# Two-layer graph network: fixed slots for the layer-1 weights, every other part with its groups in reverse, and other prefetch distances

## Chip, cores and metric

The kernel runs on 1 core of one Trainium2 chip. The metric is the device time of one execution in microseconds, given as the median of several runs. The traces come from the hardware profiler, from one execution each; "span" is the time from the first to the last instruction of that execution.

## The reference, cut

Everything is float32. `x` is (128, 128, 256): 128 batches, 128 nodes, 256 features. `adj` is (128, 128, 128).

```python
# layer 0
h = max(layernorm(x), 0)                       # over the 256 features
conv = bn(conv1d_k1(h)); conv = relu(conv); conv = bn(conv1d_k17(conv))   # along the nodes
x_conv = relu(conv + h)
s = h @ w_se.T + b_se                          # 3 values a node
A = exp(-|s_n - s_m|^2) * adj
x_nmp = A @ relu(h @ w_msg.T + b_msg)
gi = concat(x_conv, x_nmp) @ w_ih.T + b_ih;  gh = h @ w_hh.T + b_hh       # a GRU cell
x = x + (1 - z) * tanh(gi_n + r * gh_n) + z * h        # r, z = sigmoid(...)

# layer 1: only nodes 0..24 of each batch change, in five overlapping groups
GROUPS = [25 nodes], [9 nodes], [7 nodes], [6 nodes], [6 nodes]
h = max(layernorm(x), 0)
for g in range(5):
    N_g = D^-1/2 (adj_g + I) D^-1/2            # D: row sums of adj_g + I
    y = relu(N_g @ (h_g @ W1[g]) + b1[g])      # 256 -> 512
    y = relu(N_g @ (y @ W2[g]) + b2[g])        # 512 -> 256
    fused[group g] += softmax(fusion_w)[g] * y
x = x + fused
```

## The kernel before

**Layer 0.** A front part computes the convolution (up to about 640 us). Then 32 blocks of four batches follow. The function `gates(i)` computes the GRU of block i, with TensorE matmuls written out in a fixed order (L505, L541); after each it calls `between()`, which takes one step of other work: in turn a step of `beside_gates(i + 1)` (messages L411, edges L431 to L447, the inverse of the convolution L394/L396, and `back(i - 1)`) and a step of the first unfinished layer-1 generator. `back` transposes the block's result (L572), adds the residual, and stores it with one queue, SyncE's: eight small stores of the rows that layer 1 needs into scratch `xg` (L579), and then one store of the other 103 rows of each of four batches to the output (L581). The `xt` tile is loaded at L811 and has two buffers.

**Layer 1.** The 128 batches are cut into parts of 32, 32, 32, 16, 8 and 8. When a part's blocks have gone through the gates, its generator `layer1(k)` is appended; every yield of it is one step. The last parts run after the last block has been stored. Each group's rows are cut into *packs* of at most 128 rows (several batches of s rows each), and packs are put together into *chunks* of at most 512 rows. A chunk goes through these stages:

- for each pack, `prepare(j)` and then the product of the normalized rows with the adjacency (L711), copied into `ax` (L712)
- for each group segment of the chunk, the product with `w1` (L728), with bias and Relu into `hh` (L733 on VectorE, L735 on ScalarE)
- for each pack, the product with `w2` (L745), copied to `s2` (L747); `last`, one pack later, multiplies by the adjacency again (L674) and applies bias, scale and Relu (L678). Group 0 writes the sum `f`, and the other groups write `og`, which VectorE adds to `f` (L685)

After its chunks a part loads the old rows (`x1`, L761), transposes `f` (L764), adds it (L765) and stores the output (L767).

`prepare(j)` runs ahead of its pack in three distances. Loads (adjacency rows `adj`, L595, and features `hg`, L597) are five packs ahead, `pack_rows` three, `pack_adj` one:

```python
            if 0 <= j + 5 < len(packs):
                loads[j + 5] = pack_load(k, *packs[j + 5])
            if 0 <= j + 3 < len(packs):
                g, _, nb = packs[j + 3]
                rows[j + 3] = pack_rows(g, nb, *loads.pop(j + 3))
            if 0 <= j + 1 < len(packs):
                g, _, nb = packs[j + 1]
                ready[j + 1] = pack_adj(nb * GROUPS[g][0], *rows.pop(j + 1))
```

`pack_rows` computes degrees (L608 to L611), the statistics of the layernorm (L612 `st`, L613), a power on GpSimd (L615 `pw`), the normalized rows (L618, L619) and the scaled block-diagonal adjacency `bd` (L621, L624). `pack_adj` transposes it (L630) and scales it into `nt` (L632).

The weights of a group, `w1` and `w2` of 512 KB each, are loaded by SyncE (L649) in each part anew: `w1` has two buffers and `w2` three, and the next load is issued when a group has been used for the last time. With five groups and six parts that is 60 loads.

The order of the work on each engine is the program's order. Tiles wait for buffers by semaphores. All loads and stores named here go through SyncE's queue, in program order; an instruction there that waits for a buffer holds what is behind it.

Of the kernel before, what the change touches and what calls it, by code (L numbers as in the profile page):

```python
# [8 lines left out]
F32 = mybir.dt.float32  # L9
# [4 lines left out]
P = 128  # L14
# [11 lines left out]
NN = 25  # L26
HID = 512
# [15 lines left out]
    return [(b[j], b[j + 1] - b[j]) for j in range(k)]  # L43


def _chunks(size):

    out, n = [], 513
    for g, (s, _) in enumerate(GROUPS):
        for b0, nb in _packs(size, s):  # L50
            if n + nb * s > 512:
                out.append([])
                n = 0
            out[-1].append((g, b0, nb))
            n += nb * s
    return out
# [10 lines left out]
def gnn_kernel(ctx: ExitStack, tc: tile.TileContext, io, out: bass.AP):  # L67
# [359 lines left out]
    def edge_terms(i):  # L427

        ps = bank()
        for k in range(2):  # L430
            nc.tensor.transpose(ps[:, k * P:(k + 1) * P], lr[:, k].rearrange("p b r -> p (b r)"), ident)  # L431
        lt = wk.tile([P, P], F32, tag="lt", name="lt", bufs=2)
        nc.scalar.copy(lt, ps[:, :P])
        rt = wk.tile([P, BB, N], F32, tag="rt", name="rt", bufs=1)
        nc.vector.tensor_tensor(rt, ps[:, None, P:2 * P].to_broadcast([P, BB, N]),
                                bmask[32][:, :, None].to_broadcast([P, BB, N]), op=ALU.mult)
        lrs[i] = lt, rt
# [152 lines left out]
    def pack_load(k, g, b0, nb):  # L590
        s = GROUPS[g][0]
        n = nb * s
        adj = l1.tile([P, NN], F32, tag="adj", name="adj", bufs=6)
        r0 = (first_of[k] + b0) * s
        nc.sync.dma_start(adj[:n, :s], io[f"adj{g}"][r0:r0 + n, :])  # L595
        hg = l1.tile([P, D], F32, tag="hg", name="hg", bufs=6)
        nc.sync.dma_start(hg[:n], xg[k][g][b0 * s:b0 * s + n, :])  # L597
        return adj, hg

    def pack_rows(g, nb, adj, hg):  # L600

        s = GROUPS[g][0]
        n = nb * s

        deg = l1.tile([P, 5], F32, tag="deg", name="deg", bufs=4)
        st = l1.tile([P, 6], F32, tag="st", name="st", bufs=4)
        pw = l1.tile([P, 4], F32, tag="pw", name="pw", bufs=4)
        nc.vector.reduce_sum(deg[:n, 0:1], adj[:n, :s], axis=AX.X)  # L608
        nc.vector.tensor_scalar(deg[:n, 0:1], deg[:n, 0:1], 1.0, None, op0=ALU.add)
        nc.vector.tensor_scalar(deg[:n, 1:2], deg[:n, 0:1], 0.0, None, op0=ALU.is_equal)  # L610
        nc.vector.tensor_add(pw[:n, 0:1], deg[:n, 0:1], deg[:n, 1:2])  # L611
        nc.vector.bn_stats(st[:n], hg[:n])  # L612
        nc.vector.bn_aggr(deg[:n, 2:4], st[:n])  # L613
        nc.vector.tensor_scalar(pw[:n, 1:2], deg[:n, 3:4], EPS, None, op0=ALU.add)  # L614
        nc.gpsimd.tensor_tensor(pw[:n, 2:4], pw[:n, 0:2], mhalf[:n, 0:2], op=ALU.pow)  # L615
        dinv = deg[:n, 4:5]
        nc.vector.tensor_sub(dinv, pw[:n, 2:3], deg[:n, 1:2])
        nc.vector.tensor_scalar(hg[:n], hg[:n], deg[:n, 2:3], pw[:n, 3:4], op0=ALU.subtract, op1=ALU.mult)  # L618
        nc.scalar.activation(hg[:n], hg[:n], AF.Relu)  # L619
        bd = l1.tile([P, P], F32, tag="bd", name="bd", bufs=3)  # L620
        nc.vector.scalar_tensor_tensor(  # L621
            bd[:n, :n].rearrange("p (b m) -> p b m", b=nb), adj[:n, None, :s].to_broadcast([n, nb, s]), dinv,
            bmask[s][:n, :nb, None].to_broadcast([n, nb, s]), op0=ALU.mult, op1=ALU.mult)
        nc.vector.scalar_tensor_tensor(bd[:n, :n], ident[:n, :n], dinv, bd[:n, :n], op0=ALU.mult, op1=ALU.add)  # L624
        return hg, bd, dinv

    def pack_adj(n, hg, bd, dinv):
# [4 lines left out]
        nc.vector.tensor_scalar(nt[:n, :n], pt[:n, :n], dinv, None, op0=ALU.mult)  # L632
        return hg, nt

    def layer1(k):
        size = PARTS[k]
        tag = "f" if size > 8 else f"f{size}"
        f = l1.tile([P, C, size if size <= 8 else max(PARTS), NN], F32, tag=tag, name=tag, bufs=1 if size > 8 else 2)
        chunks = _chunks(size)
        packs = [p for c in chunks for p in c]  # L640
        loads, rows, ready, late = {}, {}, {}, []
        w1s, w2s = {}, {}

        def weights(ws, name, key, bufs, shape, ahead):

            while len(ws) < min(len(GROUPS), ahead):
                g = len(ws)
                ws[g] = l1.tile(shape, F32, tag=name, name=name, bufs=bufs)
                nc.sync.dma_start(ws[g], io[key][g].rearrange("(c p) o -> p c o", p=P))  # L649

        def weights1(ahead):
            weights(w1s, "w1", "w1", 2, [P, C, HID], ahead)

        def weights2(ahead):
            weights(w2s, "w2", "w2", 3, [P, HID // P, D], ahead)

        def prepare(j):

            if 0 <= j + 5 < len(packs):
                loads[j + 5] = pack_load(k, *packs[j + 5])  # L660
            if 0 <= j + 3 < len(packs):
                g, _, nb = packs[j + 3]
                rows[j + 3] = pack_rows(g, nb, *loads.pop(j + 3))
            if 0 <= j + 1 < len(packs):
                g, _, nb = packs[j + 1]
                ready[j + 1] = pack_adj(nb * GROUPS[g][0], *rows.pop(j + 1))

        def last(g, b0, nb, s2, nt):

            s, runs = GROUPS[g]  # L670
            n = nb * s
            po = bank()
            for c in range(C):
                nc.tensor.matmul(po[:, c * P:c * P + n], s2[:n, c * P:(c + 1) * P], nt[:n, :n], start=True, stop=True)  # L674
            og = None if g == 0 else l1.tile([P, C, P], F32, tag="og", name="og", bufs=2)
            for c in range(C):
                dst = og[:, c, :n] if g else f[:, c, b0:b0 + nb, :].rearrange("p b m -> p (b m)")
                nc.scalar.activation(dst, po[:, c * P:c * P + n], AF.Relu, bias=nb2[:, g, c:c + 1], scale=nw[:, g:g + 1])  # L678
            if g:
                at = 0  # L680
                ov = og[:, :, :n].rearrange("p c (b m) -> p c b m", b=nb)
                for r0, rn in runs:
                    for c in range(C):
                        fv = f[:, c, b0:b0 + nb, r0:r0 + rn]
                        nc.vector.tensor_add(fv, fv, ov[:, c, :, at:at + rn])  # L685
                    at += rn

        for j in (-5, -4):
            prepare(j)
        yield  # L690
        weights1(2)
        weights2(3)
        for _ in range(8):
            yield
        for j in (-3, -2, -1):
            prepare(j)
            yield
        ends = {g: n + 1 for n, (g, _, _) in enumerate(packs)}
        j = 0
        for chunk in chunks:  # L700
# [3 lines left out]
            for g, b0, nb in chunk:  # L704
                n = nb * GROUPS[g][0]
                prepare(j)
                hg, nt = ready.pop(j)
                j += 1
                ps = bank()
                for c in range(C):  # L710
                    nc.tensor.matmul(ps[:, c * P:c * P + n], hg[:n, c * P:(c + 1) * P], nt[:n, :n], start=True, stop=True)  # L711
                nc.vector.tensor_copy(ax[:, :, at:at + n], ps[:, :C * P].rearrange("p (c m) -> p c m", c=C)[:, :, :n])  # L712
                work.append((g, b0, nb, nt, at))
                segs[g] = (segs[g][0] if g in segs else at, at + n)
                at += n
                if late:
                    last(*late.pop(0))
                yield j + 5 >= len(packs)
            hh = l1.tile([P, HID // P, 512], F32, tag="hh", name="hh", bufs=1)
            for g, (m0, m1) in segs.items():  # L720
                m = m1 - m0
                per = 2 if m <= 256 else 1
                for q0 in range(0, HID // P, per):
# [12 lines left out]
                    if late:  # L736
                        last(*late.pop(0))
                    if q0 + per == HID // P and j >= ends[g]:
                        weights1(g + 3)
                    yield  # L740
            for m, (g, b0, nb, nt, at) in enumerate(work):
                n = nb * GROUPS[g][0]
                ps = bank()
                for q in range(HID // P):
                    nc.tensor.matmul(ps[:n, :D], hh[:, q, at:at + n], w2s[g][:, q, :], start=q == 0, stop=q == HID // P - 1)  # L745
                s2 = l1.tile([P, D], F32, tag="s2", name="s2", bufs=3)
                nc.scalar.copy(s2[:n, :], ps[:n, :D])  # L747
                if late:
                    last(*late.pop(0))
                late.append((g, b0, nb, s2, nt))  # L750
                if j0 + m + 1 == ends[g]:
                    weights2(g + 4)
                yield
        while late:
            last(*late.pop(0))
# [1 line left out]

        n = BB * NN
        for b0 in range(0, size, BB):
            x1 = l1.tile([P, D], F32, tag="x1", name="x1", bufs=3)  # L760
            nc.sync.dma_start(x1[:n], xg[k][0][b0 * NN:b0 * NN + n, :])  # L761
            ps = bank()
            for c in range(C):
# [161 lines left out]
```

## Time and profile before

| what | value |
|---|---|
| median of three runs | 2194.7 us (2188.79, 2194.7, 2196.48) |
| the profiled run | 2192.57 us, span 2190.8 us, mean TensorE clock granted 0.965 |
| TensorE matmuls, busy | 2062.6 us, 94% of the span |
| VectorE, ScalarE, GpSimd, busy | 58%, 32%, 26% |
| DMA | 260.11 MB, of which 60 weight loads of 512 KB |
| chain that ended last | TensorE 73%, DMA 12%, VectorE 8%, GpSimd 3% |

A group's row gives line, engine, operation, shapes and count, then its busy time and the mean of one instruction, and then the idle time of the engine before it with what ended it. A row of waits gives the total, how often, and the longest. A float32 matmul runs as two passes, and the trace counts passes. A busy share of the whole says little about one stretch: the stretch up to 640 us (front part), the blocks, and the time after the last block have different limits.

### The profile page before, as it was taken

The page shows a single profiled execution, that of the slowest core. Times are in us where ns is not written, and L with a number is a line of the kernel's source. Part 1 is how long each engine was busy: PE and PEld are TensorE (multiplying, and loading weights), DVE is VectorE, ACT ScalarE, POOL GpSimd, SP SyncE. Part 2 cuts the span into 40 slices and gives each one's busy share as a digit, 9 for nine tenths or more (in the row PEclk, how much of TensorE's full clock was granted, in tenths as well). Part 3 has the DMA queues.
Part 4 walks back from the last instruction along what each step waited for, and adds up shares of the span by engine and source line. Part 5 has one row for each costly group of instructions (what it writes and reads, how often), then busy time and mean ns, then how long its engine had stood idle before and what let it go on. Part 6 is the DMA issues. An engine that isn't in the chain of part 4 may idle for free.

```text
span 2190.8 us, 31132 instructions
## 1 busy us (share of the span) xinstructions
PE 2062.6 (94%) x10981; PEld 1721.8 (79%) x10981; DVE 1274.0 (58%) x3518; ACT 697.7 (32%) x1424; POOL 580.0 (26%) x666
## 2 busy tenths in 40 slices
PE   7989979998999999999999999999999999998687
PEld 6878868887778778778888877888887788886576
DVE  6666447553556556576666657656665666655332
ACT  3433114311333233333333333333333333332222
POOL 3012521143323324232222422222242222222100
PEclk8889989999999999999999999999999999999786
DMA  8974964298322222221223222122322212221252
GB/s 318 337 261 162 305 225 153 106 297 263 118 65 63 77 67 60 72 75 57 82 86 103 71 72 75 57 81 87 102 71 73 74 55 82 81 77 48 64 158 68
DMA packets 200909, 260.11 MB, mean 119 GB/s; under 512 B 19378, under 2 KB 179378, under 8 KB 196146
## 3 DMA queue, kind: packets, MB, share of 16 engines
q1 hardware_dynamic: 192946, 220.37, 31.8%
q10 hardware_dynamic: 7808, 37.75, 4.5%
q8 instruction: 88, 1.44, 0.3%
q14 instruction: 67, 0.55, 0.1%
HBM read 175.63 MB, written 82.44 MB: 118 GB/s over the span
## 4 chain that ended last, share of the span: by engine, by line
PE 73%; DMA 12%; DVE 8%; POOL 3%; SPq 1%; issue 1%; ACT 1%; POOLq 0%; DVEq 0%; ACTq 0%
PE bank L505 27%; PE bank L269 6%; PE bank L541 5%; PE bank L728 5%; DMA hg<-xg 5%; PE bank L745 4%; DMA ln<-in_x_dram 4%; PE bank L202 3%; PE bank L264 3%; PE bank L411 3%; DMA out_dram<-xt 3%; PE bank L214 3%; PE bank L457 2%; PE bank L396 2%; PE bank L394 2%; PE bank L572 1%
## 5 line engine op out<-in xcount | busy, mean ns | idle before, releaser
L505 PE MATMUL bank<-t,sw 128*128 128x256 f32 x1024 | 253.9, 381 | 1.1 <-DVE nn L520 1.1
L518 POOL TENSOR_TENSOR u<-u,m 128x256 f32<-128x256 f32 x96 | 73.1, 762 | 635.2 <-ACT m L516 611.3
L505 PEld LDWEIGHTS bank<-t,sw 128*128 128x128 f32 x1024 | 187.5, 191 | 24.6 <-DVE nn L520 1.3
L505 PE MATMUL bank<-t,wih 128*128 128x256 f32 x768 | 197.8, 380 | 0.0
L505 PEld LDWEIGHTS bank<-t,wih 128*128 128x128 f32 x768 | 145.8, 190 | 34.1 <-issue 10.7
L728 PE MATMUL bank<-ax,w 128*128 128x192 f32 (+12 forms) x592 | 131.0, 374 | 25.7 <-DMA w<-in_w_dram 22.5
L728 PEld LDWEIGHTS bank<-ax,w 128*128 128x128 f32 x592 | 105.9, 223 | 43.4 <-issue 29.4
L202 PE MATMUL bank<-wc,ht 128*128 128x256 f32 x512 | 123.9, 397 | 17.0 <-ACT ht L193 13.1
L745 PE MATMUL bank<-w,hh 128*100 128x256 f32 (+8 forms) x552 | 136.8, 394 | 0.0
L261 POOL TENSOR_TENSOR vs<-v 128x512 f32<-128x512 f32 x78 | 101.6, 1322 | 128.7 <-DMA v<-vd 78.0
L615 POOL TENSOR_TENSOR pw<-pw,mhalf 100x2 f32<-100x2 f32 (+7 forms) x69 | 50.3, 729 | 301.1 <-DVE pw L614 153.2
L411 PE MATMUL bank<-wms,ht 128*128 128x259 f32 x512 | 124.8, 387 | 4.6 <-DMA ht<-htd 4.6
L202 PEld LDWEIGHTS bank<-wc,ht 128*128 128x128 f32 x512 | 98.3, 197 | 37.4 <-ACT ht L193 22.3
L541 PE MATMUL bank<-ht,whh 128*128 128x512 f32 x256 | 116.9, 600 | 0.0
L745 PEld LDWEIGHTS bank<-w,hh 128*100 128x100 f32 (+8 forms) x552 | 94.3, 173 | 28.3
L505 PE MATMUL bank<-xc,wih 128*128 128x256 f32 x384 | 114.8, 381 | 0.0
L505 PE MATMUL bank<-xn,wih 128*128 128x256 f32 x384 | 114.7, 380 | 0.0
L411 PEld LDWEIGHTS bank<-wms,ht 128*128 128x128 f32 x512 | 98.8, 193 | 20.2 <-issue 5.0
L259 DVE SCALAR_TENSOR_TENSOR s<-X 128x256 f32<-128x256 f32 x78 | 50.8, 653 | 90.6 <-PE bank L269 90.4
L415 ACT ACTIVATE msg<-msg 128x512 f32<-128x512 f32 x64 | 40.3, 630 | 197.1 <-DVE msg L412 185.0
L214 PE MATMUL bank<-fd,h 128*128 128x160 f32 x512 | 87.8, 332 | 15.0 <-ACT h L206 12.7
L214 PEld LDWEIGHTS bank<-fd,h 128*128 128x128 f32 x512 | 83.4, 215 | 17.8 <-ACT h L206 13.1
(175 smaller groups left out, 4391.0 us busy)
## 6 DMA issues: line engine op xcount, KB each, us to landing
v<-vd SPq DMA_DIRECT2D x80, 512.0 KB
w<-in_w_dram SPq DMA_DIRECT2D x60, 512.0 KB
vd<-sp SPq DMA_DIRECT2D x8, 2560.0 KB
yd<-ys ACTq DMA_DIRECT2D x40, 512.0 KB
ln<-in_x_dram SPq DMA_DIRECT2D x32, 512.0 KB
htd<-ht ACTq DMA_DIRECT2D x32, 512.0 KB
ht<-htd SPq DMA_DIRECT2D x32, 512.0 KB
ym<-yd SPq DMA_DIRECT2D x32, 512.0 KB
```

The costliest lines, as they stand in the source:

```text
L202: nc.tensor.matmul(pv[:, bb, :], ht[:, c, b * N:(b + 1) * N], wc1[:, c, :], start=c == 0, stop=c == C - 1)
L214: nc.tensor.matmul(ps[:, bb * 2 * LW:(bb + 1) * 2 * LW], h1[:, 2 * h + bb, c * P:(c + 1) * P], fd, start=True, stop=True)
L259: nc.vector.scalar_tensor_tensor(s, a, -2.0, d, op0=ALU.mult, op1=ALU.subtract)
L261: nc.gpsimd.tensor_tensor(vs, vr, vi, op=ALU.add)
L264: nc.tensor.matmul(p1[:, :D], a[:, c], vs[:, c], start=c == 0, stop=c == C - 1)
L269: nc.tensor.matmul(ps[:, k * D:(k + 1) * D], u[:, c], w[:, c], start=c == 0, stop=c == C - 1)
L411: nc.tensor.matmul(ps[:, :D + 3], ht[:, c, b * N:(b + 1) * N], wms[:, c, :], start=c == 0, stop=c == C - 1)
L505: nc.tensor.matmul(ps, w, d, start=n == 0, stop=n == len(pairs) - 1)
L518: nc.gpsimd.tensor_tensor(got["u4"], got["u2"], got["m5"], op=ALU.add)
L541: nc.tensor.matmul(ps, whh[:, c, col:col + P], ht[:, c, :], start=c == 0, stop=c == C - 1)
L728: nc.tensor.matmul(pv[:, q - q0, :], w1s[g][:, c, q * P:(q + 1) * P], ax[:, c, m0:m1], start=c == 0, stop=c == C - 1)
L745: nc.tensor.matmul(ps[:n, :D], hh[:, q, at:at + n], w2s[g][:, q, :], start=q == 0, stop=q == HID // P - 1)
```

## The change

- The weights get three fixed slots each for `w1` and `w2`: group g lies in slot g % 3. The first part loads groups 0, 1 and 2. When a group ends, the group three further on in the present direction is loaded into its slot.
- Odd parts run through the groups from 4 down to 0, so that three groups of each kind stay in place from one part to the next. There are 30 loads instead of 60. In odd parts `f` is first set to zero by GpSimd, and group 0 is added through `og` like the others.
- `prepare` runs six packs ahead for loads, four for `pack_rows` and two for `pack_adj`. The prologue of a part has one step more.
- Buffers: `hg` 6 to 7, `adj` 6 to 4, `bd` 3 to 2, `s2` 3 to 2, `x1` 3 to 2, `lt` 2 to 1. The slots take 24 KB a partition instead of 20.

```diff
-        lt = wk.tile([P, P], F32, tag="lt", name="lt", bufs=2)
+        lt = wk.tile([P, P], F32, tag="lt", name="lt", bufs=1)
...
-        adj = l1.tile([P, NN], F32, tag="adj", name="adj", bufs=6)
+        adj = l1.tile([P, NN], F32, tag="adj", name="adj", bufs=4)
...
-        hg = l1.tile([P, D], F32, tag="hg", name="hg", bufs=6)
+        hg = l1.tile([P, D], F32, tag="hg", name="hg", bufs=7)
...
-        bd = l1.tile([P, P], F32, tag="bd", name="bd", bufs=3)
+        bd = l1.tile([P, P], F32, tag="bd", name="bd", bufs=2)
...
+    w1s, w2s = {}, {}
+
+    def weights(ws, g):
+
+        if 0 <= g < len(GROUPS):
+            name, shape = ("w1", (D, HID)) if ws is w1s else ("w2", (HID, D))
+            ws[g] = l1.tile([P, shape[0] // P, shape[1]], F32, tag=f"{name}_{g % 3}", name=name, bufs=1)
+            nc.sync.dma_start(ws[g], io[name][g].rearrange("(c p) o -> p c o", p=P))
...
-        chunks = _chunks(size)
+
+        d = -1 if k % 2 else 1
+        chunks = _chunks(size, range(len(GROUPS))[::d])
...
-            if 0 <= j + 5 < len(packs):
-                loads[j + 5] = pack_load(k, *packs[j + 5])
-            if 0 <= j + 3 < len(packs):
-                g, _, nb = packs[j + 3]
-                rows[j + 3] = pack_rows(g, nb, *loads.pop(j + 3))
-            if 0 <= j + 1 < len(packs):
-                g, _, nb = packs[j + 1]
-                ready[j + 1] = pack_adj(nb * GROUPS[g][0], *rows.pop(j + 1))
+            if 0 <= j + 6 < len(packs):
+                loads[j + 6] = pack_load(k, *packs[j + 6])
+            if 0 <= j + 4 < len(packs):
+                g, _, nb = packs[j + 4]
+                rows[j + 4] = pack_rows(g, nb, *loads.pop(j + 4))
+            if 0 <= j + 2 < len(packs):
+                g, _, nb = packs[j + 2]
+                ready[j + 2] = pack_adj(nb * GROUPS[g][0], *rows.pop(j + 2))
...
-            og = None if g == 0 else l1.tile([P, C, P], F32, tag="og", name="og", bufs=2)
+            add = g or d < 0
+            og = l1.tile([P, C, P], F32, tag="og", name="og", bufs=2) if add else None
...
-        for j in (-5, -4):
+        for j in (-6, -5):
             prepare(j)
         yield
-        weights1(2)
-        weights2(3)
+        if k == 0:
+            for g in range(3):
+                weights(w1s, g)
+                weights(w2s, g)
+        if d < 0:
+            nc.gpsimd.memset(f, 0.0)
         for _ in range(8):
             yield
-        for j in (-3, -2, -1):
+        for j in (-4, -3, -2, -1):
             prepare(j)
             yield
...
-                yield j + 5 >= len(packs)
+                yield j + 6 > len(packs)
...
-                        weights1(g + 3)
+                        weights(w1s, g + 3 * d)
...
-                s2 = l1.tile([P, D], F32, tag="s2", name="s2", bufs=3)
+                s2 = l1.tile([P, D], F32, tag="s2", name="s2", bufs=2)
...
-                    weights2(g + 4)
+                    weights(w2s, g + 3 * d)
...
-            x1 = l1.tile([P, D], F32, tag="x1", name="x1", bufs=3)
+            x1 = l1.tile([P, D], F32, tag="x1", name="x1", bufs=2)
```

## The prediction

> **What bounds the kernel now.** I read the page first, then the windows by stage, the waits (TensorE's, the whole list, SyncE's queue), the chain in order of time, and last the timeline of the ends.
>
> ```profile
> PE 2062.6 (94%) x10981; PEld 1721.8 (79%) x10981; DVE 1274.0 (58%) x3518; ACT 697.7 (32%) x1424; POOL 580.0 (26%) x666
> ```
> ```profile
> 1755.00:1974.00 219.00, 214.84 (x1101) 178.25 (x1100) 133.02 (x386) 77.90 (x155) 54.05 (x67) 1.00 0.24 74
> 1974.00:2191.00 217.00, 168.54 (x815) 138.19 (x813) 85.99 (x360) 51.43 (x132) 26.52 (x34) 0.80 0.28 84
> 2050.00:2075.00 25.00, 6.23 (x50) 5.77 (x48) 7.23 (x40) 2.88 (x8) 1.40 (x2) 0.70 0.25 77
> ```
> The columns after the stretch are its length and the busy time of PE, PEld, DVE, ACT and POOL, then the granted clock, DMA share and GB/s. TensorE sets the time: from 640 to 1974 us, where blocks of layer 0 run with layer 1 between them, the six stages sum to 1308 of 1334 us busy, so only 26 us of waiting are left there. Loose time lies at the end: 48 us of 217, of which 19 lie in the 25 us from 2050 on.
>
> ```profile
> PE bank L728 <- DMA w<-in_w_dram: 22.5, 3, 18.3
> PE bank L711 <- DVE nt L632: 15.2, 15, 1.7
> PE bank L431 <- DVE lr L424: 11.2, 8, 2.2
> ```
> These are TensorE's waits (total, times, longest). The weight wait is one hole of 18.3 us and two of 2.1; the wait for `nt` is many small ones, 13.8 us of it before 1990. SyncE's timeline shows the hole's cause:
>
> ```profile
> 2000.83 0.24 SPq L581 DMA_DIRECT2D out_dram<-xt  x1
> 2001.67 14.03 SPq L597 DMA_DIRECT2D hg<-xg  x3
> ```
> ```profile
> 2020.55 0.43 DVE L612 BATCH_NORM_STATS2 st<-hg 112x6 f32<-112x256 f32 x1 [9.78 <-DMA hg<-xg]
> 2047.96 1.09 PE L572 MATMUL bank<-ident,o 128*128 128x128 f32 x8 [0.57 <-DVE o L560]
> 2052.35 3.75 PE L728 MATMUL bank<-ax,w 128*128 128x72 f32 x32
> 2053.18 0.27 SPq L581 DMA_DIRECT2D out_dram<-xt  x1
> 2054.32 13.92 SPq L649 DMA_DIRECT2D w<-in_w_dram  x2
> 2074.44 6.56 PE L728 MATMUL bank<-ax,w 128*128 128x96 f32 x32 [18.34 <-DMA w<-in_w_dram]
> ```
> Each block ends with one store of 103 rows of 4 KB (L581, 412 KB). The `hg` load right behind the store of 2000.83 is used at 2020.55, 19.7 us later; the `w1` load behind the last store lands at 2074.4. SyncE's list has 225.6 us for the next `xt` load (L811) waiting on this store. So every block has a window of 20 to 31 us in which nothing issued behind its store arrives.
>
> **What the Trainium skill says.** "DMA: Bandwidth & Descriptors", section "Why a DMA increments its semaphore by 16 and not by 1": a transfer is spread over the largest number of engines up to 16 that divides its slowest dimension. 103 is prime, so that is one engine. The trace agrees: 412 KB in 19.6 us is 21 GB/s, while a 512 KB weight load issued clear of it (2105.64) lands in 3.8 us. "Perfetto Trace Analysis", section "Tensor Engine Instruction": VectorE and ScalarE are strict FIFO and TensorE pulls only weight loads ahead. The trace agrees: DVE idles 9.78 us at L612 though gate work stands behind it. "TensorE: Matmul & The Clock Gate", Part 1: the clock falls to half after an idle window of about 3.4 us. The granted 0.70 of 2050 to 2075 agrees.
>
> **The change part by part.** No matmul is added: L728 has 296 instructions in the order of both kernels (592 passes in the trace).
>
> *Weights.* 60 loads of 512 KB become 30. Traffic is no bound (windows: 0.23 to 0.28 of the engines), so 15.7 MB less are worth nothing by themselves; SyncE's blocked time on weight buffers (L649, 102.5 us on L728 alone) falls, but TensorE shows it only in the 22.5 us above. In the last two parts (8 batches each) a slot returns two or three groups, about 7 us, ahead of its next use, against 3.8 us to land: the waits of 2.08 and 2.04 us go.
>
> *The hole after the last transposes, T = 2047.96.* Part 3 now runs backwards; the first load behind the store is `w2` of group 0, which by queue order lands where `w1` does now, T + 26.4. But by the order of instructions TensorE has more to do first: group 0's L728 segment (400 columns, 6.0 us), other segments and four L745 packs. It arrives at T + 17 to T + 21 and waits 5 to 9 us, not 18.3. Then four packs (as in 2080.84 to 2090.12, 9.3 us), 0.9 us for the last add, as before L764, and 0.9 for extra adds: T + 37.5 to 38.5 against 43.1 now. What follows takes 99.75 us now, less 4.1. The tail is 134.5 instead of 142.8: **-8.3**.
>
> *Blocks 30 to 31.* That work leaves the 58.6 us before T: 6.0 (400 columns) + 2.0 (72 columns) + 9.5 (five L745 packs at 1.89) + 2.4 (four L674 at 0.6) = 19.9. In come segments of 112, 144 and 96 columns (8.7), one L745 pack (1.9) and one L630 (0.25). Net -9. Against that stands the wait: with adjacencies two packs ahead, the L630 transpose of pack 6 needs `bd`, and `bd` lies on VectorE behind statistics of `adj` and `hg` loaded right behind block 30's store. TensorE has 19 us of work up to it, the data comes at about 31: 12 us, against 4.9 there now. Sum **-1.9**.
>
> *The other blocks with layer 1 (8 to 29).* Two packs ahead, the transpose is no longer directly in front of its product, so most of the 13.8 us for `nt` go. In exchange, matmuls meet the window earlier: working TensorE's time from each block's transposes to the first matmul that depends on a load behind the store, I get a stall of 7 us after block 20 (need at 20.0, data at 27), 2.8 after 27, about 1.4 after 7, 22 and 23, and 0 to 1 after seven others, 17 in all. Before it is 13.8 + 2.6 (part of L431) = 16.4. Sum **+0.6**, the least certain term: the same working gives 3.0 us for block 30 before, and the trace shows 1.11 and 2.00, but elsewhere it rests on arrival times of one block. From below: all stalls but block 20's vanish and the `nt` waits go, -10. From above: 13 blocks stall 2 us more each, +26.
>
> *Buffers.* `bd` with two buffers waits for an older transpose, but the `nt` multiplication that needs it stands right behind on VectorE anyway: 0. `adj` with four, hidden under `hg` with seven, arrives with it: in the stalls above. `s2` and `lt`: the release is several matmuls old: 0. `x1` with two: add, stores and reload take about 6 us against two steps of 5.5 to 8: 0 to 1 us a part, mostly beside gates; I take 0.
>
> *Odd parts.* POOL clears `f`: 128x256 takes 0.31 us here, so 1600 columns cost about 1.9, on an engine 26% busy: 0. Group 0 goes through `og` and an add: 26 adds of 0.2 us on VectorE (58% busy), 0 but for the 0.9 counted. SyncE issues no extra DMA; past it move only `hg`/`adj` loads, one pack earlier.
>
> Sum: -8.3 - 1.9 + 0.6 = -9.6 us. The profiled span is 2190.8 (its run 2192.57); the median is 2194.7, so 2185. A measurement of this kernel tells 0.3% (6.6 us) from no change: faster is below 2188, slower above 2201.
>
> **Rivals.**
> *More gain.* Loads behind the store land nearer 20 than 31 us in most blocks, so block 30 and 20 hardly stall and the `nt` waits vanish: -8.3 - 9 - 12 = -29, about 2166. For it: `hg` loads directly behind the store land at 19.7. Against: 2074.4 in the last block.
> *No change.* TensorE reaches the new `w2` wait as early as the old one, because the packs before it depend on loads of the same window: the tail gains only the two small waits, blocks give it back, about 2193. For it: the same store, the same queue. Against: the order puts 17 us of work first.
> *Slower: one store, met sooner.* VectorE's FIFO behind the 103-row store is the mechanism in all of blocks 8 to 27 that carry layer 1 (13 of them), not in two: statistics are hoisted one pack further, so gate work queues behind them sooner, and TensorE follows. It breaks even at 9.6/13 = 0.7 us a block, is slower by over 0.3% from 16/13 = 1.25, and at 2 us gives 2211. For it: the 9.78 us VectorE already idles, and 109.9 us in all on `st` for `hg`, 26 times. Against: TensorE now idles only 1.1 and 2.0 us for it, so slack of several microseconds is there.
> *The change does nothing* is excluded: 30 loads go.
>
> **How the numbers follow.** Forecast 0.46 (2178 to 2192, some 0.07 of it above 2188), more gain 0.19, no change 0.10 (0.02 of it below 2188), slower 0.25. Faster: 0.39 + 0.19 + 0.02 = 0.60; same: 0.07 + 0.08 = 0.15; slower: 0.25. The range 2164 to 2207 takes in the forecast, no change, two thirds of more gain and half of slower; about 0.19 is left out.
>
> **What would show it.** Right: the L728 weight wait falls from 22.5 to near 0, an L745 wait of 5 to 9 us for weights appears after the last store, one of about 12 us on the adjacency transpose at 2015 to 2030, one of about 7 near block 20, and L711 on `nt` falls below 5. Wrong: 640 to 1974 us has over 45 us of TensorE idle (slower rival), or under 15 (more gain); or the hole behind the last store stays at 18 us.

## Result, and the profile after

The changed kernel takes 2214.5 us (four runs, 2211.95 to 2216.31) against 2195.6 us before (four runs, 2188.79 to 2197.58): a ratio of 1.0091, 95% interval 1.0066 to 1.0115. It is slower, and above the range that was given. It went the way of the third rival, and the time is near the one named there for two microseconds a block (2211).

The page of the changed kernel begins so. The spans of the two profiles differ by 21.1 us; TensorE is idle 14.6 us longer and busy 6.5 us longer with the same number of passes.

```profile
span 2211.9 us, 31166 instructions
...
PE 2069.1 (94%) x10981; PEld 1721.5 (78%) x10981; DVE 1286.0 (58%) x3544; ACT 699.8 (32%) x1424; POOL 574.1 (26%) x669
```

Where it went is read from the start of each block's transposes (L572, now L573) in TensorE's timeline. "After block 20" means from block 20's transposes to those of block 21. The stretches add up to the spans, but for rounding:

| stretch (us) | before | changed | difference | forecast |
|---|---|---|---|---|
| start to block 0 | 617.2 | 620.5 | +3.3 | 0 |
| block 0 to 8 (no packs of layer 1 multiplied yet) | 318.5 | 319.9 | +1.4 | 0 |
| block 8 to 29 | 1034.5 | 1063.5 | +29.0 | +0.6 |
| block 29 to 31 | 77.7 | 78.1 | +0.4 | -1.9 |
| block 31 to the end | 142.9 | 129.8 | -13.0 | -8.3 |

The first row is the front part, which the change does not aim at; over all kernels told of here it varies between 614.5 and 624.9, so 3.3 us there say nothing.

TensorE's waits of the changed kernel (total, times, longest): the long wait for `w1` is gone; waits for `w2`, for `hh` and one of 10.6 us in the transpose L631 have come; and those for `bd` have grown from 3.6 to 10.1 us.

```profile
PE bank L631 <- DVE pw L615: 10.6, 1, 10.6
PE bank L631 <- DVE bd L625: 10.1, 7, 3.8
PE bank L748 <- DMA w<-in_w_dram: 7.6, 1, 7.6
PE bank L748 <- DVE hh L736: 6.9, 1, 6.9
```

The large ones sit where the prediction put them: 10.6 and 1.5 us on the transposes after block 30 (forecast 12), 7.6 for `w2` behind the last store (5 to 9), 6.9 after block 20 (7). No wait of L714 on `nt` over 0.4 us is left. What the forecast missed shows in the windows. First the stage of blocks 17 to 21 in the kernel before, then the same stage after, and the end:

```profile
1366.00:1587.00 221.00, 217.00 (x1106) 179.14 (x1105) 134.40 (x386) 78.64 (x155) 53.47 (x67) 1.00 0.26 81
```
```profile
1375.00:1610.00 235.00, 222.59 (x1111) 181.93 (x1110) 138.39 (x386) 82.05 (x161) 51.27 (x67) 0.98 0.20 61
2082.00:2211.00 129.00, 106.35 (x522) 85.50 (x522) 46.83 (x232) 34.16 (x94) 7.31 (x11) 0.80 0.21 62
```

The stage is 14 us longer, of which 8.4 are idle. The other 5.6 are busy time: the granted clock is 0.98 instead of 1.00, and some passes more fall into the stage (1111 against 1106). From block 8 to 29 as a whole (first two lines below, before and after; the third is the time behind a stall of 2.8 us) TensorE is idle 32.3 us instead of 17.3 and busy 1031.2 instead of 1017.2, for as many columns of the product with `w1` in all, so idle time and slower passes share the loss of 29.0 in equal parts. In the kernel before no stall in this stretch is longer than 1.7 us, and the granted clock is 1.00 throughout. In the changed one seven stalls of 2.2 to 6.9 us stand there, and with each the trace shows 3.4 us at half clock (6.8 with the longest), 27.3 us in all. Half of that, 13.7 us, is an estimate of what the clock cost; it fits the 14.0.

```profile
935.72:1970.24 1034.52, 1017.23 (x5065) 834.19 (x5064) 644.44 (x1789) 358.76 (x675) 281.08 (x343) 1.00 0.25 77
```
```profile
940.46:2003.98 1063.52, 1031.22 (x5079) 841.42 (x5078) 653.28 (x1803) 360.86 (x677) 275.08 (x344) 0.99 0.21 65
1680.71:1684.11 3.40, 3.40 (x6) 1.34 (x5) 3.05 (x6) 2.26 (x4) 0.85 (x2) 0.50 0.00 0
```

Here is the longest stall, after block 20. SyncE issues the store and the `hg` load behind it, VectorE takes the statistics only 20.6 us after the store, the product with `w2` waits, and in the window around it the clock is at one half:

```profile
1555.64 0.26 SPq L582 DMA_DIRECT2D out_dram<-xt  x1
1556.33 13.52 SPq L598 DMA_DIRECT2D hg<-xg  x1
```
```profile
1576.22 0.43 DVE L613 BATCH_NORM_STATS2 st<-hg 125x6 f32<-125x256 f32 x1 [5.96 <-DMA hg<-xg]
1576.68 0.18 DVE L614 BATCH_NORM_AGGREGATE deg<-st 125x2 f32<-125x6 f32 x1
1576.78 0.66 DVE L560 TENSOR_TENSOR o<-o,z 128x512 f32<-128x512 f32 x1
1577.36 0.47 DVE L736 TENSOR_SCALAR hh<-bank,vec 128x250 f32<-128x250 f32 x1
1577.89 1.22 PE L748 MATMUL bank<-w,hh 128*125 128x256 f32 x2 [6.86 <-DVE hh L736]
```
```profile
1560.00:1570.00 10.00, 10.00 (x53) 8.99 (x52) 5.49 (x10) 3.21 (x5) 5.48 (x8) 1.00 0.07 24
1575.00:1580.00 5.00, 2.11 (x5) 1.75 (x6) 2.92 (x9) 0.37 (x1) 0.71 (x1) 0.50 0.32 109
```

The statistics of a later pack (L613) stand in front of gate work (L560) and of `hh` (L736) on VectorE, and wait for a load. From 1560 to 1570 the DMA share is 0.07 at 24 GB/s, which is about one of sixteen engines at work.

After block 11 the way leads over ScalarE. The Relu of a later pack's rows (L620) waits for its statistics and stands in front of the copy to `s2` (L750), for which TensorE waits 2.5 us:

```profile
1124.94 0.42 DVE L613 BATCH_NORM_STATS2 st<-hg 96x6 f32<-96x256 f32 x1 [4.18 <-DMA hg<-xg]
1127.29 0.42 ACT L620 ACTIVATE hg<-hg 96x256 f32<-96x256 f32 x1 [5.79 <-DVE hg L619]
1127.61 0.35 ACT L750 COPY s<-bank 112x256 f32<-112x256 f32 x1
1128.02 1.20 PE L672 MATMUL bank<-nt,s 112*128 112x112 f32 x4 [2.54 <-ACT s L750]
```

### The profile page after: what moved, and what is told of

Read it like the earlier page. It is cut to its first block, busy times and chain, and to the rows that moved or that the text cites. A ratio compares the mean times of both kernels' runs of the same rounds, so it can differ in the third digit from the quotient of the medians.

```text
span 2211.9 us, 31166 instructions
## 1 busy us (share of the span) xinstructions
PE 2069.1 (94%) x10981; PEld 1721.5 (78%) x10981; DVE 1286.0 (58%) x3544; ACT 699.8 (32%) x1424; POOL 574.1 (26%) x669
## 4 chain that ended last, share of the span: by engine, by line
PE 66%; DMA 17%; DVE 8%; POOL 5%; SPq 2%; issue 1%; ACT 1%; POOLq 0%; DVEq 0%; ACTq 0%
PE bank L506 23%; DMA hg<-xg 6%; PE bank L270 5%; PE bank L748 5%; PE bank L542 4%; PE bank L731 4%; DMA ln<-in_x_dram 4%; DMA out_dram<-xt 4%; PE bank L203 3%; PE bank L265 3%; PE bank L412 3%; PE bank L215 3%; PE bank L458 2%; PE bank L397 2%; PE bank L395 2%; DMA adj<-in_adj_dram 1%
## 5 line engine op out<-in xcount | busy, mean ns | idle before, releaser
L506 PEld LDWEIGHTS bank<-t,wih 128*128 128x128 f32 x768 | 145.4, 190 | 33.4 <-issue 10.6
L748 PE MATMUL bank<-w,hh 128*100 128x256 f32 (+8 forms) x552 | 135.5, 390 | 14.5 <-DMA w<-in_w_dram 7.6
L731 PE MATMUL bank<-ax,w 128*128 128x192 f32 (+16 forms) x592 | 129.7, 371 | 6.1 <-DVE deg L609 4.5
L616 POOL TENSOR_TENSOR pw<-pw,mhalf 100x2 f32<-100x2 f32 (+8 forms) x69 | 48.7, 707 | 327.2 <-DVE pw L612 135.9
L731 PEld LDWEIGHTS bank<-ax,w 128*128 128x128 f32 x592 | 104.1, 218 | 22.7 <-issue 11.9
```

Of the source, the lines that this page charges most:

```text
L506: nc.tensor.matmul(ps, w, d, start=n == 0, stop=n == len(pairs) - 1)
L731: nc.tensor.matmul(pv[:, q - q0, :], w1s[g][:, c, q * P:(q + 1) * P], ax[:, c, m0:m1], start=c == 0, stop=c == C - 1)
```

## Experiments

Ratios are to the kernel before on the same chip, with 95% intervals; the medians come from several chips. "Packs ahead" are the distances of loads, `pack_rows` and `pack_adj`; "steps" are those of a part's prologue until its first pack, 12 in the kernel before and 13 in the changed one. The theory at first: the distances make the loss, through the store's window. It fell, in two steps.

| kernel | median us | ratio |
|---|---|---|
| changed kernel | 2214.5 | 1.0091 (1.0066 to 1.0115) |
| changed, old distances, 12 steps | 2184.1 | 0.9957 (0.9943 to 0.9972) |
| before with the new distances, 13 steps | 2203.3 | 1.0050 (1.0030 to 1.0070) |
| changed, 6, 3, 1 packs ahead, 13 steps | 2207.0 | 1.0051 (1.0029 to 1.0073) |
| changed, 6, 3, 2 packs ahead, 13 steps | 2208.0 | 1.0064 (1.0042 to 1.0087) |
| changed, 12 steps | 2192.0 | 0.9996 (0.9982 to 1.0011) |
| changed, old distances, 13 steps | 2203.3 | 1.0049 (1.0030 to 1.0069) |
| changed, `adj` with 6 buffers | 2209.0 | 1.0067 (1.0035 to 1.0100) |
| changed, all parts forwards, old distances, 12 steps | 2183.1 | 0.9951 (0.9937 to 0.9964) |
| changed, store cut 101 + 2 | 2176.2 | 0.9929 (0.9905 to 0.9952) |
| before, store cut 101 + 2 | 2173.7 | 0.9915 (0.9883 to 0.9946) |
| changed, old distances, 13 steps, store cut 101 + 2 | 2150.3 | 0.9800 (0.9774 to 0.9825) |
| changed, store cut 96 + 7 | 2149.7 | 0.9799 (0.9777 to 0.9821) |
| before, store cut 96 + 7 | 2152.4 | 0.9822 (0.9790 to 0.9854) |
| changed, old distances, 12 steps, store cut 96 + 7 | 2138.4 | 0.9730 (0.9693 to 0.9766) |
| changed, 12 steps, store cut 96 + 7 | 2139.4 | 0.9754 (0.9723 to 0.9786) |
| changed, all parts forwards, old distances, 12 steps, store cut 96 + 7 | 2142.0 | 0.9770 (0.9743 to 0.9797) |
| changed, store cut 96 + 7, no identity in part 1 | 2145.4 | 0.9774 (0.9744 to 0.9805) |

**Distances or weights.** The changed kernel with the old distances (and 12 steps; the edit is shown without its buffers), and the kernel before with the new ones (and 13 steps):

```diff
-            if 0 <= j + 6 < len(packs):
+            if 0 <= j + 5 < len(packs):
...
-            if 0 <= j + 4 < len(packs):
+            if 0 <= j + 3 < len(packs):
...
-            if 0 <= j + 2 < len(packs):
+            if 0 <= j + 1 < len(packs):
...
-        for j in (-6, -5):
+        for j in (-5, -4):
...
-        for j in (-4, -3, -2, -1):
+        for j in (-3, -2, -1):
```

> The changed kernel with the prefetch distances of before (loads 5, pack_rows 3, pack_adj 1, with hg 6, adj 6 and bd 3 buffers); fixed weights and reversed odd parts stay. Theory (the distances cause the stalls in blocks 8 to 29): those blocks return to within 5 us of before, the gain of about 13 us after the last block stays, so 2180 to 2186. Rival (the reversed groups cause them, by putting other packs behind each block's store): blocks 17 to 25 stay 15 to 20 us longer than before and the time is 2198 to 2210.

> The kernel before with only the new distances (6, 4, 2, with hg 7, adj 4 and bd 2 buffers); weights and group order as before. Theory (distances): blocks 8 to 29 lose 20 to 28 us, the hole of 18 us after the last block stays: 2210 to 2225. Rival (reversed groups): the waits for nt go and nothing else comes, 2180 to 2192.

The first gave 2184.1, as the theory had it: 120.9 us from block 31 on, but 1052.1 from block 8 to 29, 17.6 more than before and not within 5. The second gave 2203.3, short of the range, and takes 1039.0 us from block 8 to 29, only 4.5 more than before. So the two halves of the change cost -10 and +9 us alone and +19 together: something in the distances meets something in the rest.

**Which distance.** Loads six ahead kept, `pack_rows` three, and `pack_adj` one or two ahead (the second piece of the edit belongs to the first run alone):

```diff
-                rows[j + 4] = pack_rows(g, nb, *loads.pop(j + 4))
+                rows[j + 3] = pack_rows(g, nb, *loads.pop(j + 3))
...
-                ready[j + 2] = pack_adj(nb * GROUPS[g][0], *rows.pop(j + 2))
+                ready[j + 1] = pack_adj(nb * GROUPS[g][0], *rows.pop(j + 1))
```

> The changed kernel with loads six ahead kept, and pack_rows three and pack_adj one ahead as before (adj 6, bd 3 and nt 8 buffers for it). Theory (statistics and transposes that stand earlier in the FIFOs meet the store's window; earlier loads only help): like the run with all old distances, 2176 to 2188. Rival (the loads themselves, a pack earlier in SyncE's queue, cause the loss): 2200 to 2215.

> The changed kernel with pack_rows three ahead (loads 6, pack_adj 2, adj with 6 buffers). If the hoisted statistics (pack_rows four ahead) cost the 30 us, this is near the run with 6, 3, 1: 2176 to 2190. If the transposes two ahead cost them, it stays near the changed kernel: 2203 to 2216.

2207.0 and 2208.0: the theory failed, neither hoisted statistics nor earlier transposes had to be there. But besides the load distance these two share something else with the changed kernel: its longer prologue of 13 steps. That was tried by itself, with one step less in the changed kernel (the edit shown) and one more, 9, in the one with the old distances:

```diff
-        for _ in range(8):
+        for _ in range(7):
```

> The changed kernel with 7 instead of 8 empty steps in a part's prologue, so that its packs begin after 12 steps as before and not after 13; distances 6, 4, 2 stay. Theory (the loss came with the extra step, which shifts all of a part against the blocks' stores): 2180 to 2195, and the 6.9 us before the product with w2 after block 20 falls below 4. Rival (the loads six ahead take a place in SyncE's queue that costs): 2205 to 2218.

> Fixed weights and reversed odd parts with the old distances (5, 3, 1) and 9 instead of 8 empty steps, so 13 steps. Theory (the step): 2200 to 2212, with 6 to 8 us before the product with w2 after block 20. Rival (the loads): 2178 to 2188 as with 12 steps.

2192.0 and 2203.3, with 1.7 and 7.3 us of idle time after block 20, as expected. One empty step more costs 19 to 23 us with either set of distances; the distances cost 8 to 11 us with either number of steps. This holds beside fixed slots and reversed parts: the kernel before, given 13 steps and the new distances together, lost 9 us.

**The buffers of `adj`.**

```diff
-        adj = l1.tile([P, NN], F32, tag="adj", name="adj", bufs=4)
+        adj = l1.tile([P, NN], F32, tag="adj", name="adj", bufs=6)
```

> The changed kernel with 6 instead of 4 buffers for adj. The prediction took the smaller number as nothing by itself: 2208 to 2220. If adj loads were held for a buffer and held what stands behind them on SyncE, blocks 8 to 29 get shorter: 2185 to 2205.

2209.0: no large share (VectorE's order differs in some 60 to 70 instructions here, of which more below).

**The reversal.** All parts forwards, with the weights of the next part loaded as slots come free (50 loads; the sum in the expectation is wrong), and old distances with 12 steps:

```diff
-        d = -1 if k % 2 else 1
+        d = 1
...
-                        weights(w1s, g + 3 * d)
+                        weights(w1s, next_group(k, g))
```

> Fixed weights with the old distances and 12 steps, but all parts forwards (54 - 6 = 48 loads less those that stay: groups 0, 1, 3 and 4 are loaded anew in each part, group 2 stays). If the reversal makes the gain of 21 us after the last block, the hole comes back and the time is near before, 2188 to 2198. If the fixed slots alone make it, 2180 to 2188, as with the reversal.

2183.1, as with the reversal (2184.1), but not for the reason in the expectation: forwards the wait for `w1` behind the last store is back (16.2 us), and it is made up for before. Forwards and reversed, the stretches are 1035.4 and 1052.1 us from block 8 to 29, 78.0 and 71.2 from 29 to 31, and 129.4 and 120.9 from there. So the reversal wins 15.3 us from block 29 on and loses 16.7 before. Fixed slots forwards, then reversed, then with a thirteenth step, then with the new distances, blocks 8 to 29 take 1035.4, 1052.1, 1064.5 and 1063.5 us, against 1034.5 in the kernel before: on this way the reversal and the step make the loss.

**The store's window.** The store cut in two, in the changed kernel and in the one before:

```diff
-        nc.sync.dma_start(out[i * BB:(i + 1) * BB, NN:, :].rearrange("b n d -> n b d"), xt[NN:, :, :])
+        for n0, n1 in ((NN, NN + 96), (NN + 96, N)):
+            nc.sync.dma_start(out[i * BB:(i + 1) * BB, n0:n1, :].rearrange("b n d -> n b d"), xt[n0:n1, :, :])
```

> The changed kernel with each block's store of 103 rows cut into one of 96 and one of 7 rows. Theory (loads behind a store that runs on one DMA engine arrive too late, and each stall costs a half clock on top): the stalls of 3.8, 6.9, 10.6 and 7.6 us go, with some 10 us of half clock, 2172 to 2185. Rival (VectorE has too much queued in the wrong order, whatever the loads do): the stalls in blocks 8 to 29 stay, only the 7.6 us after the last block goes, 2203 to 2210.

> The kernel before with the same cut of the store. Theory: the hole of 18.3 us and the 4.8 us of block 30 go, the waits for nt stay: 2168 to 2178. Rival (the store isn't what holds the weight load): within 5 us of before.

2149.7 and 2152.4, both below what the theory gave, and blocks 0 to 8 became 12 and 13 us shorter. Of the four stalls that the theory named for the changed kernel, those of 6.9 and 7.6 us fell to 0.8 and to nothing, that of 10.6 to 5.7, and that of 3.8 stayed (3.6). Right behind the store more DMA engines are at work now:

```profile
1530.00:1534.00 4.00, 4.00 (x27) 3.69 (x26) 2.52 (x7) 2.42 (x5) 0.00 (x0) 1.00 0.54 145
```

The control was a cut that leaves a prime number of rows in the large piece, 101 and 2:

> The changed kernel with each block's store cut into 101 and 2 rows instead of 96 and 7. 101 is prime like 103. Theory (one DMA engine takes the whole large piece): nothing changes, 2208 to 2220, and the xt load still waits some 18 us for the store. Rival (two transfers instead of one are enough): 2145 to 2170.

It came out between both: 2176.2. The store is as slow as ever (after block 20 SyncE is held 13.7 us until it has issued the second piece, and the next `xt` load is issued 19.5 us after the store, against 19.7 before the cut), the holes of 10.7 us after block 30 and 7.6 us behind the last store are still there, and yet it is 38 us faster (36 by the ratios). The orders of the two kernels in their traces tell why. TensorE's passes have the same order with and without the cut. VectorE's instructions do not: some 80 to 90 of 3,544 stand elsewhere, many of them statistics of packs; on ScalarE 4 of 1,424 do, and on GpSimd 5 of 669. (What stands ahead of the prediction, that each engine's order is the program's, is therefore wrong for these three: an edit to one DMA moved instructions that it does not touch, so the framework that builds the kernel places them anew.) The same place after block 20, in the kernel with 101 and 2 rows (its lines are one higher):

```profile
1552.69 1.21 DVE L560 TENSOR_TENSOR o<-o,z 128x512 f32<-128x512 f32 x1
1553.82 0.47 DVE L737 TENSOR_SCALAR hh<-bank,vec 128x250 f32<-128x250 f32 x1
1554.21 0.41 DVE L511 TENSOR_TENSOR z<-bank,m 128x256 f32<-128x256 f32 x1
1554.54 1.18 DVE L561 TENSOR_TENSOR o<-o,nn 128x512 f32<-128x512 f32 x1
1558.59 0.43 DVE L614 BATCH_NORM_STATS2 st<-hg 125x6 f32<-125x256 f32 x1 [2.87 <-DMA hg<-xg]
```

The statistics are taken 25.6 us after block 20's transposes (25.7 in the changed kernel), so the load comes no sooner. But `hh` now stands ahead of them, and the wait of L749 on it is 0.8 us instead of 6.9. At this place nothing else moved: of ScalarE's and GpSimd's 9 instructions none lies between 1324 and 1894 us. The cut of 96 and 7 has the same order as the cut of 101 and 2 on TensorE, VectorE, ScalarE and GpSimd, so the two differ by the store alone. Two more runs asked for the share of the order in the other kernels:

> The kernel before with the store cut into 101 and 2 rows. On TensorE, ScalarE and VectorE it has the same order as the kernel before with 96 and 7 rows, and VectorE's differs from the kernel before in 58 of 3518 instructions. Theory (where VectorE's statistics stand decides in the blocks, the one-engine store only in the hole behind the last block): blocks 0 to 8 run at 38.4 us each, the hole of 18 us stays, 2170 to 2182. Rival (the store's duration decides in both places): 2188 to 2197.

> Fixed weights, reversed odd parts, old distances, 13 steps (2203.3) with the store cut into 101 and 2 rows; VectorE's order differs in 82 of 3544 instructions, TensorE's not at all. Theory (VectorE's order): the 7.3 us before the product with w2 after block 20 fall below 2, 2164 to 2178. Rival (the extra step costs through TensorE's order): 2188 to 2203.

2173.7 and 2150.3, the first as the theory had it, the second even below its range. In stretches (us):

| kernel | block 0 to 8 | 8 to 29 | 29 to 31 | 31 to end |
|---|---|---|---|---|
| before | 318.5 | 1034.5 | 77.7 | 142.9 |
| before, 101 + 2 | 306.8 | 1031.3 | 74.3 | 145.4 |
| before, 96 + 7 | 306.8 | 1027.4 | 70.0 | 123.4 |
| changed | 319.9 | 1063.5 | 78.1 | 129.8 |
| changed, 101 + 2 | 306.8 | 1039.4 | 77.9 | 129.7 |
| changed, 96 + 7 | 306.8 | 1030.2 | 71.9 | 118.7 |
| changed, old distances, 13 steps | 320.2 | 1064.5 | 70.4 | 129.3 |
| the same, 101 + 2 | 306.8 | 1029.6 | 67.4 | 129.2 |

From block 8 to 29 the new order takes 24 us from the changed kernel, with TensorE's order and the store's speed as they were, and the faster store takes 9 more. The kernel before gains 3 and 4 there in the same way, so the distance between the two falls from 29.0 us to 8.1 with the order and to 2.8 with the faster store. The loss with 13 steps goes the same way: 1064.5 becomes 1029.6. So most of what the step cost was the cost of the order that came with it. The gain of blocks 0 to 8, 12 and 13 us, both kernels have; it is no part of the difference between them. After block 31 it is the other way round: the order gives nothing, and the faster store gives 11 us in the changed kernel and 22 in the one before.

**A VectorE instruction of 6.3 us.** With the cut into 96 and 7, the stretch from block 19's transposes to block 20's is still 65.5 us long (the expectation calls it block 20's). In this kernel as in the changed one, one VectorE instruction in it takes as long as a run of GpSimd instructions beside it. In the changed kernel, with the clock behind it:

```profile
1503.21 6.34 DVE L625 SCALAR_TENSOR_TENSOR bd<-ident,deg,bd 125x125 f32<-125x125 f32 x1
```
```profile
1503.23 0.72 POOL L525 TENSOR_TENSOR z<-u,m 128x256 f32<-128x256 f32 x1
1503.91 0.73 POOL L479 TENSOR_TENSOR t<-ht 128x256 f32<-128x256 f32 x1
...
1508.68 0.72 POOL L482 TENSOR_TENSOR t<-t,xc 128x256 f32<-128x256 f32 x1
```
```profile
1509.70 0.34 PE L631 MATMUL bank<-ident,bd 125*125 125x125 f32 x1 [3.77 <-DVE bd L625]
1510.55 1.11 PE L506 MATMUL bank<-ht,sw 128*128 128x256 f32 x2
```
```profile
1510.00:1515.00 5.00, 4.97 (x15) 3.16 (x14) 5.00 (x15) 3.12 (x4) 0.00 (x0) 0.66 0.36 108
```

L625 takes 0.34 to 0.74 us elsewhere at this size. It reads two operands from SBUF, ends 0.15 us after the ninth GpSimd instruction, and TensorE loses 3.8 us and then runs at 1.11 instead of 0.59 us for two passes. The Trainium skill ("SBUF — State Buffer", section "SBUF: two separate sides") says that such a VectorE instruction and a GpSimd one share a pair of ports, which one of them holds for its whole instruction. The rows fit that, and show more: the instruction lasted through nine GpSimd instructions that followed each other without a gap. To try it, the identity was left out of the adjacency in part 1:

```diff
+        if k != 1:
             nc.vector.scalar_tensor_tensor(bd[:n, :n], ident[:n, :n], dinv, bd[:n, :n], op0=ALU.mult, op1=ALU.add)
```

> The changed kernel with the cut store, and in part 1 alone without the second bd operation (so the identity is left out of the adjacency there). In block 19 that operation takes 6.3 us, as long as GpSimd's nine instructions beside it. Theory (two operands in SBUF wait for a port that GpSimd's uninterrupted run holds): the next VectorE instruction reads from PSUM and goes through, block 20's 65.5 us become 57 to 60, and the time is 2139 to 2145. Rival (VectorE is held there by something else): the time stays at 2147 to 2151 and another instruction takes the 6 us.

2145.4, at the edge of the theory's range; the stretch takes 59.4 us, and no VectorE instruction in the blocks is longer than 1.3 us. But the run leaves out the very instruction that was slow, and some 90 instructions of VectorE's order moved with it as well, so the port is likely and not shown to be the cause.

**Both together.**

> Fixed weights and reversed odd parts with the old distances (5, 3, 1) and the store cut into 96 and 7 rows. Theory: without the window the distances hardly matter, so this is within 8 us of the changed kernel with the cut store (2149.7) and a little below it, since the 6.3 us VectorE instruction of block 19 is not met: 2136 to 2150. Rival (the distances cost 30 us by themselves): 2115 to 2130.

> The changed kernel with the store cut into 96 and 7 rows and 12 steps. Without the window the step should matter little; what it moves is the place where VectorE's bd operation meets GpSimd's run. 2136 to 2150 (2149.7 with 13 steps); above 2155 would speak against this.

> Fixed weights, all parts forwards, old distances, 12 steps, and the store cut into 96 and 7 rows. Theory (the reversal was worth something only in the hole behind the last store): equal to or a little better than the reversed one with the cut store (2138), since VectorE has no extra adds: 2130 to 2140. Rival (the reversal fills other waits too): 2142 to 2152.

2138.4 and 2139.4, as expected, and 2142.0, outside the theory's range and at the lower end of its rival's: 2.3 to 2.7% faster than the kernel before. Their intervals overlap, so with the cut store and 12 steps neither the distances nor the reversal can be told from nothing. From block 8 to 29 the three take 1026.3, 1026.2 and 1027.5 us: the 17 us that the reversal cost there with the whole store are gone too. The thirteenth step still costs some 10 us (2149.7 against 2139.4).

## Why the prediction was wrong

- **Right:** the bound (TensorE, with a time of some 20 us behind each store in which nothing lands), and the places and sizes of the large stalls: 12.2 us after block 30 against 12, 6.9 after block 20 against 7, 7.6 for `w2` against 5 to 9, and L711's waits for `nt` gone. Two of these hits need a word. After block 30 the work and the arrival both came some 4 us later than reckoned (22.7 and 34.9 us after its transposes, against 19 and 31), and only their difference was right. After block 20 the product with `w2` needs nothing from the load: with TensorE's order and the arrival unchanged, and only the statistics moved, it waits 0.8 us. The traffic saved and the clearing of `f` show no cost. For `adj` the run with six buffers is 5 us below, its interval reaching to the changed kernel's; the zero stands roughly. `s2`, `lt` and `x1` were not tried by themselves.
- **After block 31: -8.3 forecast, -13.0 measured.** The wait was right: part 3's last transposes (L767) begin 38.1 us after T (2082.1 here), inside the 37.5 to 38.5. (With these the prediction's own parts give -8.7 to -9.7; the -8.3 does not follow from them.) What comes after took 91.7 us instead of 95.6: TensorE is busy 76.5 us there instead of 80.9, for 382 passes instead of 380, and the granted clock is 0.77 instead of 0.72, which the sum left out.
- **Blocks 30 to 31: -1.9 forecast, about nothing measured** (58.6 and 58.8 us). The wait came; the half clock around it was not counted.
- **The step that failed: "The other blocks with layer 1 (8 to 29) ... Sum +0.6".** It measured +29.0. The term was mis-sized in two ways. First, the stalls: TensorE's idle time is 32.3 us there, not 17 (it was 17.3 before). The working looked for matmuls that depend on a load behind the store. It missed work that does not, but stands behind that load's statistics on VectorE or behind their Relu on ScalarE: `s2` after block 11 (2.5 us), and `lr` after block 22 (2.8 instead of 1.4). It also missed 2.2 us each after blocks 8 and 24, where the product with `w1` waits for `ax`, whose copy L715 comes late on a busy VectorE with no load waited for (the list names L609, the next instruction behind that copy), and 3.8 after block 19 (`bd`, beside GpSimd's run). Except for `lr`, nothing or at most 1 us had been counted for these. Second, the price of a stall: the prediction quoted the Trainium skill on the clock ("TensorE: Matmul & The Clock Gate", Part 1) and yet counted a stall as its idle time alone. That put at nothing a term that measured 14.0 us of busy time.
- **What a stall cost.** The changed kernel and the same with 101 + 2 run the same passes in the same order, so their stretches can be compared one by one. After blocks 11, 20, 22 and 27 idle time of 2.5, 6.0, 2.8 and 1.8 us went, and the stretch became 4.3, 7.9, 4.6 and 3.3 us shorter: 1.5 to 1.9 us more than the idle time, where a stall of 2.5 to 6.9 us had stood. Where stalls of 1.0 to 1.6 us went (after blocks 0, 3, 6, 15 and 23), it became 0.2 us shorter than that. Two stalls of 2.2 us lie on the border: with that after block 4 went 1.9 us more, with that after block 2 only 0.2. The prediction took an idle window of about 3.4 us from the skill's page on the clock; here five stalls of 2.2 to 2.8 us between blocks 8 and 29 came with 3.4 us at half clock each, and the measurement decides.
- **The rival that came true** is the third: statistics hoisted on VectorE, gate work behind them, TensorE after it. Its mechanism is shown by the cut of 101 and 2. That its number is near is chance: it reckoned 26 us of idle time spread over 13 blocks, and there are 15, of which 6.4 fall to the stretch after block 20, with as much again through the clock. The sign named for it, over 45 us idle from 640 to 1974 us, was not met (40.9). Its cause was not "hoisted one pack further": the run with `pack_rows` three ahead loses nearly as much. VectorE's order was taken as a property of the distances; it follows from everything that shifts the steps. The largest shifts were the reversal (16.7 us from block 8 to 29 with the old distances) and the extra step of the prologue (12.4 more), for which the sum has no term.
- **Open:** by what rule VectorE's order is chosen was not tried, so it can't be said beforehand which edit makes it better. No run changes the order and nothing else: in the cut kernels a small store also stands behind the large one, and 9 instructions of ScalarE and GpSimd moved too. That the order does it rests on the unchanged arrival of the load after block 20, where only the statistics moved. The 8.1 us that stay between the two kernels with 101 + 2 from block 8 to 29 are spread over several stretches and were not taken apart; the largest piece, 3.8 us, is after block 19, where the instruction of 6.3 us stands in the changed kernel alone.

## What to carry to other kernels

When an edit shifts when work is issued, compare the order of each engine before and after, and look for instructions that wait for a load and stand in front of work the bounding engine needs. In this kernel their place mattered more than the time at which the load came. Do not price a TensorE stall at its idle time alone: here one of 2.5 us or more cost 1.5 to 1.9 us on top, while those of 1.0 to 1.6 us cost 0.2 us on top. Look at every large store's row count: 103 rows ran on one DMA engine for some 19.5 us and held what was queued behind it, and cutting that store into 96 and 7 took some 40 us from the kernel before, where fixed weights with the old distances took 10.

## What was not expected

- A change of one DMA (101 and 2 rows), with the same engine working as long, moved 36 to 38 us. As far as the runs show it did so through the order of VectorE, with a few instructions of ScalarE and GpSimd.
- SyncE itself is held behind a one-engine store. After block 20 the issue of the `hg` load took 13.5 us, and with 101 and 2 rows the second piece of 2 rows was held as long. Whatever stood next (`hg`, `w`, `adj` or a store), its issue ended 13.6 to 14.5 us after the store's; only the next `xt` load waits for the store itself.
- One VectorE instruction of 0.34 to 0.74 us took 6.3 us beside nine GpSimd instructions in a row.
